# A graph layer and a mixture of experts on one core: seven stages to a row tile in place of ten, a new order of the three products and of the norms' shift, small loads of their own, and another way to the power of e

## The chip, the core and the metric

The kernel runs on one NeuronCore of a Trainium2 chip. The core has five engines with instruction queues of their own: PE (TensorE, matrix products), DVE (VectorE), ACT (ScalarE), POOL (GpSimd) and SP (SyncE, which here only issues DMAs). Each works through its queue in order and waits on semaphores for the others. A weight load of PE (PEld) can run beside a product. Sixteen DMA engines move data between HBM and the on-chip memory.

The metric is the device time of one execution in microseconds (us); lower is better. Times are medians of several runs. The profile is of one further execution, taken by the hardware profiler.

## What is computed

Two layers over 6,250 nodes with 512 features each, in f32. Cut to what matters:

```python
def gnn(x, src, dst):                       # x: layer-normed rows
    agg = segment_sum(x[src], dst)          # 106,250 edges, sorted by dst
    h = (agg / max(cnt, 1)) @ W_l.T + b_l + x @ W_r.T
    h = (h - mean(h, 0)) * rsqrt(var(h, 0) + EPS) * gamma + beta
    return relu(h) + x

def ffn(t):                                 # t: layer-normed rows
    logits = gelu(t @ Wg1 + bg1) @ Wg2 + bg2
    gates = softmax(logits)
    topv, topi = top_k(gates, 2)            # two of eight experts
    topv = topv / sum(topv)
    cw = sum(one_hot(topi) * topv)
    h = gelu(ln(t @ W1[e] + b1[e]) * g1[e] + be1[e])     # 512 -> 256, for each expert e
    h = gelu(ln(h @ W2[e] + b2[e]) * g2[e] + be2[e])     # 256 -> 256
    o = h @ W3[e] + b3[e]                                # 256 -> 512
    return sum_e(cw[:, e] * o[e])

x = x + gnn(layernorm(x), src, dst)
x = x + ffn(layernorm(x))
```

## The kernel before

**Graph layer.** Rows are normed and stored in HBM, gathered by edge with indirect DMAs (L636), summed per node by products with a selection matrix (L643), multiplied by W_l and W_r (L432) and stored as `d_d`. Column sums give the factors `bn_a` and `bn_b` of the norm over all nodes. Nothing of this is touched by the change.

**Expert layer.** The 49 token tiles of 128 nodes are cut into seven groups of seven. A token tile is loaded (`token_load`), scaled by `bn_a` and shifted by `bn_b` on DVE (`token_scale`, L822 and L823); its input row is normed on ACT (`token_shift`, L828); DVE adds the two and takes the statistics (`token_sum`, L834, L784, L785); ACT norms it (`token_norm`, L804); PE transposes it (`token_turn`, L846) and computes the gate's first product (`token_gate`, L855), ACT its gelu (L857), PE the logits (`token_logits`, L864). When a group has its logits, `route` chooses two experts for each token, computes their two weights with an exponential on ACT (L919, L920, L932 to L934), and assigns each token a row in a *row tile*: 128 rows of one expert in `xs_d`, 528 numbers each (512 features, the token's number, eight weights, padding). `send` scatters the rows there with indirect DMAs on POOL (L868). `route` is a generator in pieces, which are placed in chosen steps.

A full row tile is a *job*; up to 105 are provided for, 102 of them in the ordinary course and the last three behind a flag. Per job:

- `job_load` (L1071, SP): the row tile comes in, 128 x 528
- `job_turn` (L1077 to L1088): DVE copies the token numbers (`to`, as integers) and the weight of this expert (`cw`) out of the tile; PE transposes it in four parts; ACT copies the result to `xT`
- `layer(p, 0)` and `layer(p, 1)` (L1096, L1099, L784, L785): the product with W1 or W2 on PE, then on DVE the bias and the statistics of the norm
- `layer_norm` (L804, ACT), `layer_turn` (L1113 on PE, L1116 on ACT): the norm, its transposes, the gelu with gain and shift
- `job_product` (L1125, PE), `job_bias` (L1132, DVE), `job_weigh` (L1136, ACT): the product with W3, its bias, the weight
- `job_out` (L1140, POOL): an indirect DMA that adds the rows to `out`

**Order.** It is written out by hand in `run(s, ...)`: step s handles one stage each of several jobs and token tiles. `on(lag)` means job s - lag, `at(lag)` a token tile that entered `lag` steps ago. A job is transposed in step s; W1 follows in s + 1, the norm in s + 2, its transposes in s + 3, W2 in s + 4, norm in s + 5, transposes in s + 6, W3 in s + 7, bias and weighing in s + 8 and the scatter in s + 9. In a step's end PE runs W1, W2, W3 in this order. The order of the calls in `run` is the order in each engine's queue.

The statistics of a step's two layer outputs and its token tile lie together in one small tile `mv` of a `Step`. `scales()` adds the epsilon on DVE (L794) and raises to the power -1/2 on POOL (L795); `shifts()` computes minus mean times scale on DVE in the next step (L799). Both numbers feed ACT's norms (L804). In `run` the shifts stand behind `token_scale`, `token_shift` and `token_sum`.

Buffers: four tiles `xe`, fourteen of `to` and `cw`, three of `oe` (the output rows), three of `hn` for each layer; in PSUM three banks for transposes, two halves for W1 and W2 and one bank for W3. `no_tokens` fills a tile with zeros and the number 65536 (`OOB`), which the scatter leaves out; it is written to the empty slot `xs_d[SLOTS]` once (L1283).

Ahead of the steps `ahead` brings the first two groups of tokens through, without jobs beside them.

Of the kernel before, what the change touches and what calls it, by code (L numbers as in the profile page):

```python
# [28 lines left out]
def gnn_moe_kernel(ctx: ExitStack, tc: tile.TileContext, x, src, dst, wlT, b_l, wrT, gamma, beta,  # L29
# [736 lines left out]
    def no_tokens(a):  # L766

        nc.vector.memset(a, 0.0)
        nc.vector.memset(a[:, D:D + 1], OOB)
        return a  # L770

    JOBS = {}
# [47 lines left out]
    def token_scale(q, j):  # L820
        dt = tokens[q, j][1]
        nc.vector.tensor_mul(dt, dt, bn_a)  # L822
        nc.vector.tensor_add(dt, dt, bn_b)  # L823

# [57 lines left out]
    def route(q):  # L882
# [36 lines left out]
        nc.vector.tensor_tensor(s[:, 2:4], s[:, 0:2], s[:, None, 0].to_broadcast([P, 2, n]), op=OP.subtract)  # L919
        nc.scalar.activation(s[:, 2:4], s[:, 2:4], AF.Exp)  # L920
# [4 lines left out]
        nc.vector.tensor_copy(t2[:, :n, D], tok[:, g[0]:g[0] + n])  # L925
# [140 lines left out]
    def job_load(p):  # L1066
        sl, e = JOBS[p]
        at = nc.values_load(sl, engines=[SP_], min_val=0, max_val=SLOTS,
                            skip_runtime_bounds_check_because="a tile's number, or SLOTS")
        xe = sb.tile([P, RW], F32, name="xe", bufs=4)  # L1070
        ld = nc.sync.dma_start(xe, xs_d[ds(at, 1)].rearrange("o p c -> p (o c)"))  # L1071
        tc.add_to_no_dep_group("full", ld.ins)
        XE[p] = xe

    def job_turn(p):
        xe = XE.pop(p)
        e = nc.values_load(JOBS[p][1], engines=[PE_, DVE_, ACT_], min_val=0, max_val=E - 1,  # L1077
                           skip_runtime_bounds_check_because="an expert's number")
        to = sb.tile([P, 1], I32, name="to", bufs=14)
        cw = sb.tile([P, 1], F32, name="cw", bufs=14)  # L1080
        nc.vector.tensor_copy(to, xe[:, D:D + 1])
        nc.vector.tensor_copy(cw, xe[:, D + 1:D + 1 + E][:, ds(e, 1)])
        EV[p] = e, to, cw
        pt = ps.tile([P, KD, P], F32, name="pt", bufs=3)
        for k in range(KD):
            nc.tensor.transpose(pt[:, k, :], xe[:, k * P:(k + 1) * P], ident)  # L1086
        XT[p] = sb.tile([P, KD, P], F32, name="xT")
        nc.scalar.copy(XT[p], pt)  # L1088
# [49 lines left out]
    def job_out(p):  # L1138
# [4 lines left out]
        tc.add_to_no_dep_group("added", st.ins)  # L1143

# [51 lines left out]
    def run(s, prev, lo, hi, moves=False, do=(), late=()):  # L1196
# [73 lines left out]
    with tc.manual_schedule():  # L1270
# [95 lines left out]
        for s in range(MOST, MOST + 10):  # L1366
            prev = run(s, prev, 0, MOST)
    with tc.If(flag > 0), tc.manual_schedule():
        prev = Step()
        for s in range(MOST, SLOTS + 10):  # L1370
# [38 lines left out]
```

## Time and profile before

| | |
|---|---|
| time of the runs | 2033.29 us median of 3 (2033.22 to 2036.03) |
| the profiled execution | 2240.89 us, span 2239.1 us |
| granted clock of TensorE | 0.937 mean |
| graph layer | to about 1433 us |
| first two token groups | to 1514.0 us, when the first row tile is transposed |
| steps with jobs | 1514.0 to 2228.8 us (last scatter) |
| PE busy | 1925.0 us of the span; 647 of the 725 us from 1514.0 on |
| DVE, ACT, POOL busy | 1090.2, 666.7, 1208.0 us of the span |
| job scatter on POOL (L1140) | 102 of 1.63 us |
| power on POOL (L795) | 121 of 0.87 us |
| copies of numbers and weights on DVE (L1081, L1082) | 102 each of 0.154 us |
| table loads on ACT (L920, L1116, L857) | 7 + 5 + 3 of 1.28 us |

The profiled execution is 207.6 us longer than the median of the runs. How to read the profile: "busy" is the time in which an engine had an instruction of its own; a product of PE is counted to its modelled end. A row `PE pt L846 <- ACT t L804: 11.2, 5, 2.8` in the waits says that PE's transposes of line 846 waited for ACT's line 804 for 11.2 us in all, 5 times, 2.8 us at most. In the chain of waits a row is start, length and what. In a timeline it is start, length, engine, line and operation, and in brackets how long the engine was idle before it and what ended that. In the rows by stage ("windows") the busy times of PE, PEld, DVE, ACT and POOL come first, with the instructions in brackets, then the granted clock, the share of DMA and its GB/s.

### The profile page before, as it was taken

To read this page: it belongs to the slowest core of one execution; us is meant where nothing else is said; L and a number is where in the kernel's file an instruction comes from. 1 tells how busy PE (TensorE), PEld (TensorE's weight loads), DVE (VectorE), ACT (ScalarE), POOL (GpSimd) and SP (SyncE) were. 2 spreads that over 40 slices of the span, in tenths; PEclk is the share of its full clock that TensorE was granted. 3 is DMA by queue.
4 is the path that set the end of the run, shared out by engine and by line. 5 is a ranking of instruction groups with operands and counts; after the bars stand their busy time and mean duration, and the time that the engine had idled before them with its cause. 6 is when DMAs were issued, how large, how long until landed. Compare 5 with 4: busy or idle time off the path is not lost. (4 is left out here: it accounts for less than half of the span.)

```text
span 2239.1 us, 23976 instructions
## 1 busy us (share of the span) xinstructions
PE 1925.0 (86%) x6268; PEld 1048.7 (47%) x6268; DVE 1090.2 (49%) x2577; ACT 666.7 (30%) x1284; POOL 1208.0 (54%) x1229
## 2 busy tenths in 40 slices
PE   6867988889889988998988988657899999998993
PEld 2433433334334433444443443336676766766761
DVE  5642333333333333333333333477878787785652
ACT  3420000000000000000000000255676776765662
POOL 1346666556566666666666666143455454465342
PEclk9989999899999999999999999767999999999997
DMA  7876677666667777777877766465667676655542
GB/s 249 274 269 201 211 214 207 199 196 193 192 192 214 231 228 213 229 230 235 278 231 223 252 205 195 138 217 180 162 159 196 144 204 156 178 135 125 96 68 36
DMA packets 183185, 434.09 MB, mean 194 GB/s; under 512 B 32484, under 2 KB 38638, under 8 KB 182626
## 3 DMA queue, kind: packets, MB, share of 16 engines
q0 software_dynamic: 91040, 274.90, 45.4%
q1 hardware_dynamic: 91606, 156.69, 21.0%
q8 instruction: 56, 0.92, 0.2%
q10 hardware_dynamic: 396, 0.87, 0.1%
q14 instruction: 87, 0.71, 0.1%
HBM read 331.22 MB, written 104.20 MB: 194 GB/s over the span
## 5 line engine op out<-in xcount | busy, mean ns | idle before, releaser
L636 POOL DMA_INDIRECT xg<-xn_d,scol x832 | 790.1, 950 | 465.7 <-PE pa L643 198.4
L643 PE MATMUL pa<-xg,sel 128*128 128x512 f32 x1664 | 813.3, 612 | 21.6 <-issue 19.6
L643 PEld LDWEIGHTS pa<-xg,sel 128*128 128x128 f32 x1664 | 316.4, 197 | 378.0 <-issue 370.0
L1140 POOL DMA_INDIRECT out<-oe,to x102 | 166.7, 1634 | 189.4 <-DMA out<-oe,to 33.6
L507 DVE TENSOR_SCALAR rc<-pt 128x1 f32<-128x1 f32 x49 | 7.7, 158 | 474.4 <-PE pt L586 248.4
L432 PE MATMUL ph<-wl,xT 128*128 128x512 f32 x392 | 201.1, 596 | 14.4 <-issue 11.0
L1096 PE MATMUL pm<-w1s,xT 128*128 x816 | 207.6, 399 | 3.6 <-DVE hn L1099 3.6
L1125 PE MATMUL po<-w3s,hT 128*128 x408 | 198.0, 608 | 12.7 <-DVE oe L1132 12.5
L795 POOL TENSOR_TENSOR mv<-mv,mhalf 128x2 f32<-128x2 f32 (+2 forms) x121 | 105.6, 872 | 190.7 <-DVE mv L794 187.7
L562 DVE TENSOR_REDUCE ss<-sel 128x128 f32<-128x2304 f32 x49 | 199.4, 4069 | 0.5 <-issue 0.4
L528 ACT ACTIVATE sq<-dt 128x512 f32<-128x512 f32 x49 | 29.5, 602 | 569.2 <-issue 356.2
L432 PE MATMUL ph<-wr,xT 128*128 128x512 f32 x200 | 122.4, 698 | 68.7 <-ACT xT L427 45.8
L1096 PEld LDWEIGHTS pm<-w1s,xT 128*128 128x128 f32 x816 | 154.1, 199 | 23.8 <-DVE hn L1099 4.6
L1116 ACT ACTIVATE hT<-pt,gbe 128x128 f32<-128x128 f32 x408 | 153.9, 461 | 1.5 <-PE pt L1113 1.4
L567 ACT ACTIVATE ag<-pa,rc 128x512 f32<-128x512 f32 x49 | 33.7, 687 | 380.4 <-PE pa L643 263.6
L804 ACT ACTIVATE hn<-hn,mv 128x256 f32<-128x256 f32 x204 | 112.0, 601 | 101.7 <-DVE mv L799 101.1
L432 PEld LDWEIGHTS ph<-wl,xT 128*128 128x128 f32 x392 | 73.5, 190 | 113.5 <-issue 106.4
L556 DVE TENSOR_TENSOR sel<-jrow_p,dcol 128x2304 f32<-128x2304 f32 x49 | 124.4, 2539 | 0.0
L868 POOL DMA_INDIRECT xs_d<-t,pos x98 | 101.1, 1032 | 41.7 <-issue 25.0
L427 ACT COPY xT<-pt 128x512 f32<-128x512 f32 x74 | 43.3, 585 | 231.0 <-PE pt L425 64.7
L1125 PEld LDWEIGHTS po<-w3s,hT 128*128 128x128 f32 x408 | 76.1, 192 | 76.6 <-issue 54.4
L524 DVE TENSOR_TENSOR dt<-ph,xo 128x512 f32<-128x512 f32 x24 | 16.6, 691 | 189.1 <-issue 106.4
(307 smaller groups left out, 2236.3 us busy)
## 6 DMA issues: line engine op xcount, KB each, us to landing
xe<-xs_d SPq DMA_DIRECT2D x102, 264.0 KB
xg<-xn_d,scol POOLq DMA_INDIRECT x832
d_d<-dt SPq DMA_DIRECT2D x49, 256.0 KB
dt<-d_d SPq DMA_DIRECT2D x49, 256.0 KB
xt<-in_x SPq DMA_DIRECT2D x24, 512.0 KB
xn_d<-xt SPq DMA_DIRECT2D x24, 512.0 KB
xy<-y_d SPq DMA_DIRECT2D x48, 256.0 KB
xt<-in_x SPq DMA_DIRECT2D x48, 256.0 KB
```

The costliest lines, as they stand in the source:

```text
L432: nc.tensor.matmul(p, xT[:, k, :], w[:, k, :], start=start and k == 0, stop=stop and k == KD - 1)
L556: nc.vector.tensor_tensor(SEL[t], jrow_p[:, None, :].to_broadcast([P, KS, P]), dcol[:, t // TG, (t % TG) * KS:(t % TG + 1) * KS, None].to_ ...
L562: nc.vector.tensor_reduce(ss, SEL[t].rearrange("p k j -> p j k"), AX.X, OP.add)
L636: nc.gpsimd.indirect_dma_start(out=xg, out_offset=None, in_=xn_d[:, :], in_offset=bass.IndirectOffsetOnAxis(ap=scol[:, t // TG, c:c + 1], ...
L643: nc.tensor.matmul(PA[t], SEL[t][:, k, :], xg, start=(k == 0), stop=(k == last))
L795: nc.gpsimd.tensor_tensor(self.part[:, :, 1], self.part[:, :, 1], mhalf[:, :hi - lo], op=OP.pow)
L804: nc.scalar.activation(out_, in_, AF.Identity, bias=scale_shift[1], scale=scale_shift[0])
L868: st = nc.gpsimd.indirect_dma_start(out=xs_d.rearrange("n p c -> (n p) c"), out_offset=bass.IndirectOffsetOnAxis(ap=at, axis=0), in_=rows_ ...
L1096: nc.tensor.matmul(pm, lhs[:, k, :], w[:, k, ds(e, 1), :].rearrange("p o h -> p (o h)"), start=(k == 0), stop=(k == kk - 1))
L1116: nc.scalar.activation(hT[:, k, :], pt[:, k, :], AF.Gelu, bias=gb[:, 2 * i + 1:2 * i + 2], scale=gb[:, 2 * i:2 * i + 1])
L1125: nc.tensor.matmul(po, hT[:, k, :], w3s[:, k, ds(e, 1), :].rearrange("p o h -> p (o h)"), start=(k == 0), stop=(k == KH - 1))
L1140: st = nc.gpsimd.indirect_dma_start(out=out[:, :], out_offset=bass.IndirectOffsetOnAxis(ap=to[:, 0:1], axis=0), in_=OE.pop(p), in_offset=N ...
```

## The change

- A job passes in seven steps: W1 in the step of its transposes, W2 in the step of the first norm's transposes, W3 with bias and weighing one step behind the second norm's transposes, the scatter one step later. The last loops have 7 further steps in place of 10.
- In a step PE runs W3 (with its bias on DVE queued behind it), then W1, then W2; W3 comes ahead of the norms, W1 and W2 stay at the end.
- `token_scale` is split: `token_mul`, then both `shifts()`, then `token_add` and `token_sum`. On ACT `token_shift` comes behind the norms and the weighing.
- Numbers and weights of a job have a DMA of their own into a tile `ev` of 16 columns (14 buffers), and `xe` keeps the 512 features. The token's number is stored as an integer, so that the scatter reads it where it lies; ACT picks the expert's weight itself. The two DVE copies fall away.
- `route` needs one power for each token: e to the second logit minus the first, on POOL, with a tile full of e as the base; the first weight's numerator is 1.
- The empty tile is made in a buffer of the token rows (`t2s[1]`) in place of an `xe` tile.

```diff
     def no_tokens(a):
         nc.vector.memset(a, 0.0)
-        nc.vector.memset(a[:, D:D + 1], OOB)
+        nc.vector.memset(a[:, D:D + 1].bitcast(I32), int(OOB))
         return a
+    euler = wts.tile([P, GMAX], F32, name="euler")
+    nc.vector.memset(euler, 2.718281828459045)
...
-    def token_scale(q, j):
+    def token_mul(q, j):
         dt = tokens[q, j][1]
         nc.vector.tensor_mul(dt, dt, bn_a)
+
+    def token_add(q, j):
+        dt = tokens[q, j][1]
         nc.vector.tensor_add(dt, dt, bn_b)
...
-        nc.vector.tensor_tensor(s[:, 2:4], s[:, 0:2], s[:, None, 0].to_broadcast([P, 2, n]), op=OP.subtract)
-        nc.scalar.activation(s[:, 2:4], s[:, 2:4], AF.Exp)
+        nc.vector.tensor_sub(s[:, 3], s[:, 1], s[:, 0])
+        nc.gpsimd.tensor_tensor(s[:, 3], euler[:, :n], s[:, 3], op=OP.pow)
...
-        nc.vector.tensor_copy(t2[:, :n, D], tok[:, g[0]:g[0] + n])
+        nc.vector.tensor_copy(t2[:, :n, D].bitcast(I32), tok[:, g[0]:g[0] + n])
...
-        nc.vector.tensor_add(s[:, 0], s[:, 2], s[:, 3])
-        nc.vector.reciprocal(s[:, 1], s[:, 0])
-        nc.vector.tensor_tensor(s[:, 2:4], s[:, 2:4], s[:, None, 1].to_broadcast([P, 2, n]), op=OP.mult)
+        nc.vector.tensor_scalar(s[:, 0], s[:, 3], 1.0, None, op0=OP.add)
+        nc.vector.reciprocal(s[:, 2], s[:, 0])
+        nc.vector.tensor_mul(s[:, 3], s[:, 3], s[:, 2])
...
-        xe = sb.tile([P, RW], F32, name="xe", bufs=4)
-        ld = nc.sync.dma_start(xe, xs_d[ds(at, 1)].rearrange("o p c -> p (o c)"))
-        tc.add_to_no_dep_group("full", ld.ins)
-        XE[p] = xe
+        xe = sb.tile([P, D], F32, name="xe", bufs=4)
+        ev = sb.tile([P, RW - D], F32, name="ev", bufs=14)
+        for a, lo, hi in ((xe, 0, D), (ev, D, RW)):
+            ld = nc.sync.dma_start(a, xs_d[ds(at, 1), :, lo:hi].rearrange("o p c -> p (o c)"))
+            tc.add_to_no_dep_group("full", ld.ins)
+        XE[p] = xe, ev
...
-        to = sb.tile([P, 1], I32, name="to", bufs=14)
-        cw = sb.tile([P, 1], F32, name="cw", bufs=14)
-        nc.vector.tensor_copy(to, xe[:, D:D + 1])
-        nc.vector.tensor_copy(cw, xe[:, D + 1:D + 1 + E][:, ds(e, 1)])
-        EV[p] = e, to, cw
+        EV[p] = e, ev[:, 0:1].bitcast(I32), ev[:, 1:1 + E][:, ds(e, 1)]
...
-        for i, lag in ((0, 3), (1, 6)):
+        for i, lag in ((0, 2), (1, 4)):
             if on(lag):
                 layer_turn(s - lag, i)
-        if on(9):
-            job_out(s - 9)
-        if on(8):
-            job_bias(s - 8)
+        if on(6):
+            job_out(s - 6)
         if moves:
             if at(5):
                 token_logits(*at(5))
             if at(1):
-                token_scale(*at(1))
-                token_shift(*at(1))
+                token_mul(*at(1))
+        tprev.shifts()
+        prev.shifts()
+        if moves:
+            if at(1):
+                token_add(*at(1))
             if at(2):
                 token_sum(*at(2), step)
-        tprev.shifts()
-        prev.shifts()
-        for lag in (2, 5):
+        if on(5):
+            job_product(s - 5)
+            job_bias(s - 5)
+        for lag in (1, 3):
             if on(lag):
                 layer_norm(s - lag)
         if moves and at(3) and at(3) != normed_one:
             token_norm(*at(3))
-        if on(8):
-            job_weigh(s - 8)
+        if on(5):
+            job_weigh(s - 5)
+        if moves and at(1):
+            token_shift(*at(1))
         for f in do:
             f()
-        if on(1):
-            layer(s - 1, 0, step)
-        if on(4):
-            layer(s - 4, 1, step)
-        if on(7):
-            job_product(s - 7)
+        if on(0):
+            layer(s, 0, step)
+        if on(2):
+            layer(s - 2, 1, step)
...
-                no = sb.tile([P, RW], F32, name="xe", bufs=4)
-                nc.sync.dma_start(xs_d[SLOTS], no_tokens(no))
+                nc.sync.dma_start(xs_d[SLOTS], no_tokens(t2s[1][:, 0, :]))
...
-        for s in range(MOST, MOST + 10):
+        for s in range(MOST, MOST + 7):
             prev = run(s, prev, 0, MOST)
```

More of the change, by code (lines that the diff above doesn't have):

```diff
@@ L818, in token_load, with token_scale @@
         tokens[q, j] = xt, dt
-    def token_scale(q, j):
+    def token_mul(q, j):
         dt = tokens[q, j][1]
         nc.vector.tensor_mul(dt, dt, bn_a)
+    def token_add(q, j):
+        dt = tokens[q, j][1]
         nc.vector.tensor_add(dt, dt, bn_b)
+    def token_scale(q, j):
+        token_mul(q, j)
+        token_add(q, j)
     def token_shift(q, j):
@@ L1069, in job_load @@
                             skip_runtime_bounds_check_because="a tile's number, or SLOTS")
[L1070 to L1073 removed]
+        xe = sb.tile([P, D], F32, name="xe", bufs=4)
[4 more added lines that the diff above has]
+        XE[p] = xe, ev
     def job_turn(p):
[L1076 removed]
+        xe, ev = XE.pop(p)
         e = nc.values_load(JOBS[p][1], engines=[PE_, DVE_, ACT_], min_val=0, max_val=E - 1,
                            skip_runtime_bounds_check_because="an expert's number")
[L1079 to L1083 removed]
+        EV[p] = e, ev[:, 0:1].bitcast(I32), ev[:, 1:1 + E][:, ds(e, 1)]
         pt = ps.tile([P, KD, P], F32, name="pt", bufs=3)
@@ L1369, in gnn_moe_kernel @@
         prev = Step()
-        for s in range(MOST, SLOTS + 10):
+        for s in range(MOST, SLOTS + 7):
             prev = run(s, prev, MOST, SLOTS)
```

## The prediction

> **What bounds the kernel now.** I read the rows by stage first (the windows view), because the share of busy time over the whole span mixes two kernels: the graph layer up to about 1433 us, which the change does not touch, and the expert layer behind it. In the expert layer the steps that carry a job run from the first transposes of a row tile at 1514.0 to the last scatter at 2228.8.
>
> ```profile
> 1604.30:1990.00 385.70, 363.17 (x1743) 261.03 (x1742) 312.91 (x1052) 277.36 (x569) 197.34 (x170) 0.98 0.68 172
> 1990.00:2043.60 53.60, 45.24 (x197) 31.04 (x196) 32.12 (x113) 30.63 (x67) 38.76 (x36) 0.99 0.62 149
> 2043.60:2239.10 195.50, 160.95 (x670) 110.44 (x670) 95.49 (x307) 105.73 (x233) 75.34 (x63) 0.91 0.44 75
> ```
>
> The columns behind the length are PE, PEld, DVE, ACT, POOL busy, then the granted clock. In the middle PE is busy 363 of 386 us, so most steps are at PE's own pace. The chain of waits gives that pace: W1 begins at 1622.52, 1629.77 and 1637.03, so 7.25 us with a token tile; in the timeline the transposes of xe stand at 2062.00 and 2067.18, so 5.18 us without. Fourteen jobs and seven token tiles make 14 x 5.18 + 7 x 2.07 = 87.0 us of PE. But the chain shows one restart after a stall per group, at 1614.92, 1711.50, 1808.59 and 1904.53: 96.5 us apart. **9.5 us per group are not PE's work.** The waits of PE in 1604.3 to 1990 name them:
>
> ```profile
> PE pt L846 <- ACT t L804: 11.2, 5, 2.8
> PE pt L1113 <- ACT hn L804: 3.1, 3, 1.1
> PE pt L1086 <- issue: 3.1, 4, 1.2
> PE pm L1096 <- DVE hn L1099: 2.5, 2, 2.2
> PE po L1125 <- DVE oe L1132: 2.2, 5, 0.6
> ```
>
> 22.1 us in four groups, mostly for ACT's norms (L804). What makes ACT late stands in the chain itself:
>
> ```profile
> 1702.39 0.69 DVE oe L1132
> 1703.08 0.61 DVE dt L822
> ...
> 1703.72 0.69 DVE dt L823
> 1704.41 0.61 DVE xt L834
> ...
> 1705.04 0.71 DVE st L784
> 1705.75 0.02 issue
> 1705.77 0.07 DVE mv L785
> ...
> 1705.87 0.14 DVE mv L799
> ...
> 1706.04 1.09 ACT hn L804 x2
> 1707.13 0.71 ACT t L804
> ...
> 1707.89 1.01 PE pt L846 x4
> ```
>
> The 0.14 us shift (L799), which the norms need, stands on DVE behind 3.5 us of bias and token work, and PE's transposes wait at the end of that row. Last, POOL's timeline of the end:
>
> ```profile
> 2208.27 1.59 POOL L1140 DMA_INDIRECT out<-oe,to  x1 [3.26 <-ACT hT L1116]
> 2213.91 1.53 POOL L1140 DMA_INDIRECT out<-oe,to  x1 [4.05 <-DMA out<-oe,to]
> 2219.29 1.53 POOL L1140 DMA_INDIRECT out<-oe,to  x1 [3.85 <-DMA out<-oe,to]
> 2224.68 1.54 POOL L1140 DMA_INDIRECT out<-oe,to  x1 [3.85 <-DMA out<-oe,to]
> ```
>
> Each scatter into out is issued only when the one before has landed. From 2180.73 to 2224.68 that is 8 in 43.95 us, 5.49 us each, and from 2109.38 to 2155.24, with row tiles still being loaded, 5.73. This is slower than PE's 5.18: **from about 2109 on the end is set by how many scatters are left.**
>
> **The change part by part.**
>
> *Seven stages for ten.* A job's scatter goes out in the sixth step behind its transposes, where it was the ninth. No work is added or removed; 111 steps become 108. In the tail three more scatters are already out when the last job enters: 3 x 5.49 = **-16.5 us**. If the scatters did not bind, three drain steps would go all the same, at 4 to 5 us each by an estimate from PE's 5.18 with a job or more missing (13 us), so this part is safe within 4 us.
>
> *W3, W1, W2, and use in the same step.* W1 now needs xT of the same step, W2 needs hT of the same step. Cover: between the transposes of xe and W1 PE has those of hn (0.44) and W3 (1.72), 2.16 us, and ACT's copy takes 0.58, so 1.5 us are spare; the first two of the four gelus (1.51 for four) have W1's 1.74 us besides. W3 has its bias a whole step before the next W3, so the 2.2 us for "oe" go. In the first five steps W3 is not there yet and W1 waits about 0.6 us for the copy, 3 us at most; DVE paces these steps, so I cost it at nothing. W2 and W3 also come into the filling earlier, with their additions (1.05 us of DVE for one, 0.69 for the other) in 2 and 3 steps: +4.2 at most on DVE.
>
> *The shift ahead of the token work.* Multiply, then shifts, then add, sum and bias. Of the 3.5 us ahead of L799 only one 0.69 us operation is left, so ACT's norms come up to 2.8 us sooner; the longest stall was 2.8. On ACT the token's own shift (0.82) moves behind the norms and the weighing; its reader on DVE comes in the next step. On DVE the bias now waits for W3, and the routing pieces and both hn additions are queued behind it, which PE's next W1 and the norms need. In a token step DVE begins some 1.3 us after the end of W2 (addition and statistics of hn1) and has 3.2 us of token work, so it comes to the bias after 4.5; W3 ends after 0.44 + 0.98 + 0.59 + 0.44 + 0.31 + 1.72 = 4.5 us of PE. The wait is short. What is late next is DVE itself: 312.9 us busy of 385.7, with waits of only 13 us in a group of 97. I let the waits for t, hn and oe go, 11.2 + 3.1 + 2.2 = **-16.5 us**, and leave the other 5.6. Bounds: 0 to -22.
>
> *The clock behind the stalls.* In 1711.3 to 1716.0 the granted clock was 0.62, and twelve W1 and W2 matmuls took 4.32 us where full steps take 2.79. PE is busy 363.2 us in four groups whose work is 348, so 15 us are slow matmuls. The Trainium skill (TensorE: Matmul & The Clock Gate, "What's actually happening") lets the clock fall after an idle window of about 3.4 us; the waits of PE here are at most 2.8 us, and by that rule nothing slowed and nothing comes back: 0. The row shows that it slowed. I follow the row, but take half: **-8 us**.
>
> *Numbers and weights from a load of their own.* DVE loses two copies, 0.154 us each (102 + 102), which gives back 0.36 us per step in its order (1689.40 to 1689.76 in the timeline); this is what lets DVE follow PE and is not counted again. SP issues one more DMA a step (about 0.35 us; it idles), with rows of 64 bytes. "DMA: Bandwidth & Descriptors" ("Bandwidth") speaks against it: a transfer of 4 KB costs 0.68 us and small ones are all descriptors; an estimate of 0.7 us for each of some 20 loads beside binding scatters would be +14. The row: a whole 264 KB load delays a scatter by 5.73 - 5.49 = 0.24 us, so a 8 KB one by no more, at most +5. I take **+1.5**.
>
> *The power of e on POOL.* Seven exponentials on ACT and 15 table loads of 1.28 us (7 + 5 + 3) go: 19 us of an ACT that is busy 277 of 386. POOL gains seven powers of seven columns; by the rows (0.86 us at 2, 0.93 at 3, 1.04 at 4 columns) about 1.35 us each. The result is read a step later; POOL waits 83 us for DVE in the middle stage. Behind it on POOL stand the step's own power and then a scatter, which both wait for later work. Nothing, and -2 us ahead of the steps.
>
> *Filling and last group.* In 1514 to 1604 PE waits 8.8 us for ACT's t and hn and for oe; against the +4.2 above I take -3. In 1990 to 2043.6 PE waits 5.8 us for the first row tile of the last group, which stays, and 2.8 for hn and oe: -2.
>
> The empty tile written from another buffer and the integer in place of a float cost nothing: the same bytes, far from any wait.
>
> **Sum:** -16.5 - 16.5 - 8 + 1.5 - 2 - 3 - 2 = -46.5 us on an execution of 2240.9 (span 2239.1): about 2194. The runs shown have a median of 2033.3, 207.6 us less, and no view says where. If the gain shrinks with them (x 0.907) it is -42; if not, -46.5. I take -43: **1990 us**.
>
> **Rivals.**
> 1. *DVE stays the limit.* For it: DVE is busy 78 of 97 us in a group and waits 13, so with the gaps between instructions 84 us are its own. The stall then moves from the norms to the hn additions, and only the tail is won, with a few us of the rest: 2033 - 16.5 - 4 = **2013**. Against it: 0.36 x 14 = 5 us of DVE go per group.
> 2. *PE alone is left.* All four groups at 87: 4 x 9.5 = 38, tail 16.5, filling and last group 12: **1967**. Against it: routing makes single steps too long for DVE.
> 3. *Slower: W1 waits for ACT.* One mechanism: in token steps ACT ends with weighing, token shift, copy of tt and gelu, and only then copies xT. The timeline shows ACT idle 0.9 us ahead of xT in such steps, and the cover adds 1.5. If the token shift, now behind the weighing, which itself waits for the bias, makes ACT later by over 2.4 us, each of about 33 token steps pays the rest. At 3.9 us late that is 33 x 1.5 = 50, the groups' gain is lost, and the tail's remains: 2033 - 16.5 + 50 = **2067**. It makes the kernel slower than before from 2.9 us on. Against it: 5.92 us of ACT work in a step of 7.3.
>
> **The numbers.** Forecast 0.50, rival 1 0.18, rival 2 0.15, rival 3 0.17. About 4 us (0.2%) is what a measurement can tell from no change; I give 0.03 of rival 1 and 0.02 of rival 3 to that. Faster 0.80, same 0.05, slower 0.15. The range takes in the forecast, rival 2 with its bounds and most of rival 1: 1958 to 2032.
>
> **What would show it.** Groups of 14 jobs 89 to 92 us apart; no wait of the token transposes for ACT's t over 1 us; granted clock 1.00 in all steps from 1600 on; first scatter some 20 us earlier and the same 5.5 us between the last ones; no table load behind the first gelu. I am wrong if PE's W1 waits for ACT's xT, or DVE's hn waits vanish while PE's appear, or if the spacing of the last scatters grows with the small loads.

## The result, and the profile after

The changed kernel takes 2042.85 us (median of 15 runs, 2038.13 to 2051.72); the kernel before, on the same chip, 2033.29. The ratio is 1.0048, 95% interval 1.0034 to 1.0061. The prediction was 1990 us: the change costs about 9.6 us where it was to save 43. Here and below a ratio leaves out executions in a slower state of the chip, so it can differ by up to 0.4% from the quotient of two medians.

Two lengths show where the time went. From the first transposes of job 0 to those of job 77, the profile of before has 529.6 us (1514.0 to 2043.6), that of after 557.0 (1310.4 to 1867.4): 27.4 us more. From there to the end of the last scatter before has 186.7, after 168.8: 17.9 us less. The sum is +9.5. That it fits the times so well is luck: a second profile of the changed kernel gave 550.5 and 165.8, together 716.3 us, no longer than before, though that kernel's runs were slower again (1.0042). The expert part of single profiles varies by some 5 to 10 us, so the verdicts below rest on the times, and profiles tell where to look.

The view by stages, four groups of 14 jobs each. First before, the last row of the answer for jobs 14 to 70; then after, row by row. The columns behind the length are PE, PEld, DVE, ACT and POOL busy, then the granted clock.

```profile
sum 384.00, PE 365.02 PEld 262.12 DVE 312.35 ACT 276.69 POOL 197.40; mean PE 91.26 PEld 65.53 DVE 78.09 ACT 69.17 POOL 49.35
```

```profile
1411.50:1514.40 102.90, 94.18 (x441) 65.40 (x439) 73.93 (x234) 67.30 (x140) 53.52 (x45) 0.97 0.67 169
1514.40:1615.80 101.40, 92.80 (x440) 64.73 (x438) 74.64 (x234) 67.03 (x140) 49.87 (x44) 0.98 0.65 166
1615.80:1717.20 101.40, 91.68 (x440) 63.64 (x439) 74.72 (x234) 67.03 (x140) 51.16 (x44) 1.00 0.66 166
1717.20:1820.60 103.40, 93.04 (x437) 65.37 (x436) 75.02 (x250) 65.21 (x138) 51.45 (x46) 0.97 0.59 145
sum 409.10, PE 371.70 PEld 259.14 DVE 298.30 ACT 266.57 POOL 206.01; mean PE 92.92 PEld 64.79 DVE 74.58 ACT 66.64 POOL 51.50
```

A group takes 102 us, not the 89 to 92 of the prediction. DVE and ACT did lose work (312 to 298, 277 to 267 us), as the change says. But PE now stands still for 37.4 of 409.1 us, before for 19.0 of 384.0 (34.5 of 399.6 in the second profile). The engines that were thought late have less work, and PE waits more. (PE's busy time is 6.7 us longer too; the second profile does not show that, 365.1.) The waits of PE in these four groups of after:

```profile
PE pt L855 <- ACT t L806: 11.4, 12, 2.1
PE pt L1120 <- ACT tt L857: 9.8, 11, 1.7
PE pl L938 <- DVE t L935: 5.1, 4, 1.5
PE po L1132 <- DVE oe L1139: 3.8, 3, 1.3
PE pm L1103 <- DVE hn L1106: 3.5, 5, 2.3
PE pt L1120 <- ACT hn L806: 2.4, 8, 0.6
```

The wait for ACT's t, the first that was to go, is still there (11.4 us in 12 waits). A new one stands beside it: PE's transposes wait for ACT's copy tt, 9.8 us. Behind both are waits of DVE and of ACT, in the same stretch:

```profile
ACT hn L806 <- DVE mv L801: 65.5, 35, 4.9
...
DVE mv L801 <- POOL mv L797: 55.8, 46, 3.9
...
ACT oe L1143 <- DVE oe L1139: 33.9, 36, 2.8
...
DVE oe L1139 <- PE po L1132: 16.3, 8, 4.3
```

In before, over the same jobs, DVE's wait for the power and ACT's for the shift (lines 795 and 799 there) were shorter, and the two waits with oe did not show at all:

```profile
DVE mv L799 <- POOL mv L795: 4.9, 5, 1.4
...
ACT hn L804 <- DVE mv L799: 37.3, 24, 3.9
```

One step of after in the order of time:

```profile
1441.78 1.63 POOL L1147 DMA_INDIRECT out<-oe,ev  x1 [4.02 <-ACT oe L1143]
...
1442.88 0.17 DVE L796 TENSOR_SCALAR mv<-mv 128x3 f32<-128x3 f32 x1
...
1443.71 1.03 POOL L877 DMA_INDIRECT xs_d<-t,pos  x1 [0.30 <-issue]
...
1443.74 1.98 PE L1132 MATMUL po<-w3s,hT 128*128 x4
...
1445.04 0.99 POOL L877 DMA_INDIRECT xs_d<-t,pos  x1 [0.30 <-issue]
...
1446.03 0.93 POOL L797 TENSOR_TENSOR mv<-mv,mhalf 128x3 f32<-128x3 f32 x1
...
1446.99 0.17 DVE L801 SCALAR_TENSOR_TENSOR mv<-mv 128x3 f32<-128x3 f32 x1 [3.94 <-POOL mv L797]
...
1447.19 1.09 ACT L806 ACTIVATE hn<-hn,mv 128x256 f32<-128x256 f32 x2 [1.96 <-DVE mv L801]
...
1448.71 0.69 DVE L1139 TENSOR_TENSOR oe<-po,b3s 128x512 f32<-128x512 f32 x1
...
1449.04 0.66 PE L855 MATMUL pt<-identx,t 128*128 128x128 f32 x4 [0.73 <-ACT t L806]
...
1449.44 0.72 ACT L1143 ACTIVATE oe<-oe,ev 128x512 f32<-128x512 f32 x1 [0.45 <-DVE oe L1139]
```

DVE has the variance ready at 1443.05, but POOL has a scatter and two sends ahead of the power. The power comes at 1446.03, and the shift, now ahead of the token work, holds DVE for 3.94 us. ACT's norms wait 1.96 us for it, and PE's transposes of t 0.73 us in the end. This row is what first suggested the cause, and the experiments show that it was mostly not the cause. The same rows show the bias (L1139): W3 ends at 1445.72, DVE comes to its bias at 1448.71 without a wait for W3, and ACT's weighing (L1143) waits 0.45 us for that bias.

The tail did about what was predicted. The last scatters of after on POOL:

```profile
2014.63 1.59 POOL L1147 DMA_INDIRECT out<-oe,ev  x1 [3.33 <-ACT hT L1123]
...
2020.05 1.59 POOL L1147 DMA_INDIRECT out<-oe,ev  x1 [3.21 <-ACT hT L1123]
2025.31 1.54 POOL L1147 DMA_INDIRECT out<-oe,ev  x1 [3.67 <-issue]
2030.77 1.53 POOL L1147 DMA_INDIRECT out<-oe,ev  x1 [3.92 <-issue]
```

They still follow one another at 5.2 to 5.5 us. Three steps fewer saved 17.9 us here and 20.9 in the second profile, somewhat more than three such distances.

### The profile page after: what moved, and what is told of

It reads as the page before. It is cut to its first block, busy times and chain, and to the rows that moved or that the text cites. A ratio compares the mean times of both kernels' runs of the same rounds, so it can differ in the third digit from the quotient of the medians.

```text
span 2044.7 us, 24373 instructions
## 1 busy us (share of the span) xinstructions
PE 1864.5 (91%) x6268; PEld 1025.6 (50%) x6268; DVE 1060.8 (52%) x2370; ACT 649.1 (32%) x1263; POOL 1226.3 (60%) x1234
## 5 line engine op out<-in xcount | busy, mean ns | idle before, releaser
L643 PE MATMUL pa<-xg,sel 128*128 128x512 f32 x1664 | 789.9, 597 | 20.2 <-DMA y_d<-xg 18.5
L643 PEld LDWEIGHTS pa<-xg,sel 128*128 128x128 f32 x1664 | 306.5, 191 | 365.4 <-issue 349.1
L1147 POOL DMA_INDIRECT out<-oe,ev x102 | 167.8, 1645 | 155.0 <-ACT hT L1123 45.6
L1132 PE MATMUL po<-w3s,hT 128*128 x408 | 203.4, 622 | 6.0 <-DVE oe L1139 6.0
L1103 PE MATMUL pm<-w1s,xT 128*128 x816 | 198.9, 387 | 8.5 <-DVE hn L1106 6.7
L526 DVE TENSOR_TENSOR dt<-ph,shift 128x512 f32<-128x512 f32 x25 | 17.3, 692 | 192.3 <-PE ph L432 192.3
L1103 PE MATMUL pm<-w2s,hT 128*128 x408 | 105.9, 382 | 0.0
L432 PE MATMUL ph<-wr,xT 128*128 128x512 f32 x200 | 102.1, 592 | 0.0
```

The costliest lines, as they stand in the source:

```text
L432: nc.tensor.matmul(p, xT[:, k, :], w[:, k, :], start=start and k == 0, stop=stop and k == KD - 1)
L643: nc.tensor.matmul(PA[t], SEL[t][:, k, :], xg, start=(k == 0), stop=(k == last))
L1103: nc.tensor.matmul(pm, lhs[:, k, :], w[:, k, ds(e, 1), :].rearrange("p o h -> p (o h)"), start=(k == 0), stop=(k == kk - 1))
L1132: nc.tensor.matmul(po, hT[:, k, :], w3s[:, k, ds(e, 1), :].rearrange("p o h -> p (o h)"), start=(k == 0), stop=(k == KH - 1))
L1147: st = nc.gpsimd.indirect_dma_start(out=out[:, :], out_offset=bass.IndirectOffsetOnAxis(ap=to[:, 0:1], axis=0), in_=OE.pop(p), in_offset=N ...
```

## The experiments

In the first and third batch the chips gave 2229 and 2232 us for the kernel before, in the others 2032 to 2038; the extra 200 us lie in the graph layer. So a run is judged by its ratio to before on its own chip, and the intervals of the first and third batch are wider.

### First batch: one part undone at a time

The letters in the expectations name explanations of the loss; each is told where it first appears. The three parts other than the stages were put back one at a time, each as it was in before. The shift behind the token sum:

```diff
             if at(1):
                 token_mul(*at(1))
-        tprev.shifts()
-        prev.shifts()
-        if moves:
             if at(1):
                 token_add(*at(1))
             if at(2):
                 token_sum(*at(2), step)
+        tprev.shifts()
+        prev.shifts()
```

> The changed kernel with one part undone: the norms' shifts stand on DVE behind the token sum again (token multiply, add and sum first), all else stays. Changed kernel 2042.8, before 2033.3. Theory A (the shift, put ahead of the token work, makes DVE wait for POOL's power, which stands on POOL behind the scatters: 56 us in four groups that the token work hid before): groups of 14 jobs come back from 102 us to about 97, time 2015 to 2022. Theory B (the loss is in SP's and POOL's loop, by the second small load, or in W3's bias, and the place of the shift only moves the wait to another name): 2038 to 2050. If the shift ahead was a gain as predicted: 2055 or more.

One load of 528 columns per job, with DVE's two copies:

```diff
-        for a, lo, hi in ((xe, 0, D), (ev, D, RW)):
-            ld = nc.sync.dma_start(a, xs_d[ds(at, 1), :, lo:hi].rearrange("o p c -> p (o c)"))
+        ld = nc.sync.dma_start(xe, xs_d[ds(at, 1)].rearrange("o p c -> p (o c)"))
...
+        nc.vector.tensor_copy(to, xe[:, D:D + 1].bitcast(I32))
+        nc.vector.tensor_copy(cw, xe[:, D + 1:D + 1 + E][:, ds(e, 1)])
```

> The changed kernel with one part undone: one load of 528 columns per job and DVE's two small copies of it (token number, weights) as before, all else stays. Theory A (shift ahead of POOL): 2042 to 2052, since the two copies come back on DVE. Theory B (the second load on SP, 0.5 us of SP in a loop from the sends' landing over the row load and the token store to the next scatter): up to 0.5 us less in each of some 70 steps against 0.25 us more on DVE: 2015 to 2030.

The exponentials on ACT:

```diff
-        nc.gpsimd.tensor_tensor(s[:, 3], euler[:, :n], s[:, 3], op=OP.pow)
+        nc.scalar.activation(s[:, 2:4], s[:, 2:4], AF.Exp)
```

> The changed kernel with one part undone: the two exponentials of the gate on ACT again (with its table loads), the sum of both numerators on DVE; all else stays. Theory A (shift): 2040 to 2048, no change. Theory C (the power of e blocks POOL's queue until DVE's two maxima are there: 3.5 us in each of 5 groups, and PE waits 1.3 us for the routing product): 2025 to 2036.

And one edit that no part of the change made, on SP's queue. In both kernels the token store stands behind the loads of job rows:

```diff
-        loads(min(s + 4, hi))
+        loads(min(s + 1, hi))
         if on(0):
             job_turn(s)
...
                 token_sum(*at(2), step)
+        loads(min(s + 4, hi))
```

> The changed kernel with SP's order changed: a step's token store is issued ahead of the loads of job rows of that step, which wait on SP for the landing of the sends. The scatter of a job waits for the landing of the store of the step before (13.8 us of POOL waits in four groups, and what stands behind it). Theory A with this loop (late store, late scatter, late sends, late power, late shift, late store): the power comes 1 to 3 us earlier in most steps, 2015 to 2032. If the loop does not matter: 2040 to 2046.

Measured against before (2229.18 us there): shift back 2231.67, ratio 1.0021 (0.9997 to 1.0044); one load 2245.23, 1.0061 (1.0036 to 1.0085); exponentials on ACT 2237.79, 1.0030 (1.0009 to 1.0051); store first 2227.32, 0.9982 (0.9956 to 1.0008). Of the three undone parts, only the shift's interval leaves out the changed kernel's own 1.0048, and just so. That edit gave some 6 us where theory A (the early shift is the loss) expected 20 to 28, though its profile shows DVE's wait for the power down from 55.8 to 24.4 us:

```profile
DVE mv L801 <- POOL mv L797: 24.4, 27, 1.1
DVE oe L1139 <- PE po L1132: 13.8, 12, 1.7
...
DVE hn L1106 <- PE pm L1103: 12.9, 15, 1.1
```

Much of DVE's wait only changed its name. Theory B (the second load on SP) expected 13 to 28 us from the one load, and it is no faster; C (the power of e holds POOL) expected 7 to 18 us from ACT's exponentials, and gave some 4 with an interval that takes in none. The load order on SP was the one clear gain over the changed kernel (0.9982 against 1.0048); against before its interval does not exclude no change.

### Second batch: the stages alone

> The changed kernel itself, as a control beside the others: its expert part (first transposes of job 0 to the end of the last scatter) took 725.8 us in its one profile, 716.3 in the one of before. The graph layer ahead of it differs by tens of us between executions and between chips, so the expert part is what is compared. Expected: 723 to 729 us, ratio to before 1.003 to 1.006.

For the stages alone all three parts above were undone together.

> The changed kernel with three of its four parts undone: shifts behind the token sum, one load of 528 columns with DVE's two copies, exponentials on ACT. What is left is seven stages in place of ten, W3 ahead of W1 and W2. Theory A (the shift ahead is the loss, the others near nothing): expert part 705 to 717 us, thus not slower than before (716.3). Theory D (the seven stages themselves make the groups longer: the bias in the same step as its product, the gelu tiles needed at once): 718 to 730 us.

In the next one the two sends of a step go behind its power on POOL:

```diff
         step.scales()
+        for f in end:
+            f()
         return step
...
-                    put(do, a + j * (b + 1 - a) // g, send, q + 1, j)
+                    put(rows_late, a + j * (b + 1 - a) // g, send, q + 1, j)
```

> The changed kernel with the two sends of a step issued on POOL behind the step's power in place of ahead of it; the shift stays ahead of the token work, the scatter stays where it is. Theory A (DVE waits for a power that stands behind 2 x 1.0 to 1.3 us of sends): the 14 us per group of DVE's wait shrink in the steps with sends, expert part 706 to 718 us. If the power is late for another reason than what stands ahead of it on POOL: 722 to 728 us.

The last has the edit of SP's order above, made to the kernel before.

> The kernel before with only SP's order changed: token store ahead of the step's loads of job rows. In before the late store is hidden (POOL waits 5.3 us for it in four groups, DVE waits 4.9 us for the power). Theory A (the loop hurts only where the shift stands ahead of the token work): 712 to 717 us for the expert part, ratio 0.997 to 1.001. If the loop through the store cost before as much as it costs after: 690 to 700 us, ratio 0.990.

Measured (before 2032.16): the changed kernel again 2040.17, 1.0042 (1.0025 to 1.0058); **stages alone 2040.22, 1.0046 (1.0030 to 1.0062)**; sends behind 2045.98, 1.0068 (1.0051 to 1.0086); before with the store first 2026.76, 0.9970 (0.9960 to 0.9981).

The seven stages in their order, with a late shift, one load and ACT's exponentials, lose as much as the whole change: the other three parts together are worth nothing that this can tell. Theory A falls as the main cause, D (the seven stages in their order are the loss) stands. That rests on the times: the expert parts of the single profiles, 716.3 us for the changed kernel again and 715.1 for the stages alone, were expected at 723 to 729 and, by D, at 718 to 730; they missed both, and 715.1 lies in A's range. The waits in the groups of the stages alone, of DVE, PE and, in the last row, ACT:

```profile
DVE mv L801 <- POOL mv L797: 15.6, 31, 1.6
...
DVE oe L1141 <- PE po L1134: 14.2, 14, 1.7
DVE hn L1108 <- PE pm L1105: 13.4, 17, 1.5
...
PE pt L855 <- ACT t L806: 14.4, 10, 3.0
PE pt L1122 <- ACT hn L806: 8.7, 8, 2.6
PE pl L938 <- DVE t L935: 5.4, 4, 1.6
...
ACT oe L1145 <- DVE oe L1141: 2.8, 7, 0.4
```

Here DVE waits about a quarter as long for POOL, and PE still waits 14.4 us for t. ACT's wait for oe is down from 33.9 to 2.8 us, and the time is the same: that row of the changed kernel is not the loss by itself. With the sends out of the power's way DVE's wait for it fell only to 41.2 us, and a wait for the loads of d_d of 23.0 us came up: a miss for theory A too. The store ahead of the loads was expected to give 0 to 4 us on before by theory A, and about 20 if it cost as much there as in after; it gave 5.4. So the late store costs before as well, and there the row to see it in was DVE's 4.9 us for the power: with the store first it is gone.

### Third batch: W3 behind W2 again

If it is the order in the step, then it can be put back without giving up a stage, by taking W3's product one job earlier:

```diff
         if on(6):
             job_out(s - 6)
+        if on(5):
+            job_bias(s - 5)
...
-        if on(5):
-            job_product(s - 5)
-            job_bias(s - 5)
...
             layer(s - 2, 1, step)
+        if on(4):
+            job_product(s - 4)
```

The four runs are the stages alone and the whole change, each with this edit, without and with the store first.

> The seven stages alone (as in the run with the three other parts undone, ratio 1.0046), with one change: W3's product goes back behind W2's, one job earlier, and its bias opens the next step, so that it is still seven stages. Theory E (the order W3, W1, W2 puts W2's product last: it ends 6.1 us into a step of 7.1 in place of 4.2 of 6.9, and the chain from its end over DVE's statistics, POOL's power and the shift takes 4.1 us, so the next step waits for it): groups back to 95 to 97 us with the shorter tail kept, ratio 0.988 to 0.995 (2008 to 2022 us). Theory F (fewer stages as such: each product needs what ACT makes in the same step): groups stay at 98 to 102 us, ratio 1.002 to 1.008.

> The whole change, with W3's product behind W2's and the bias at the head of the next step (seven stages, shift ahead, small loads, power of e all kept). Theory E: DVE's wait for the power, 46 to 56 us in four groups, falls below 25, ratio 0.986 to 0.995. Theory A (the early shift behind POOL's scatters costs by itself, whatever stands behind W2): ratio 1.000 to 1.005, slower than the seven stages alone with W3 last. Theory F: 1.002 to 1.008.

> The whole change with W3 last, and the token store ahead of the step's loads on SP. Theory E, with the store's loop (6 us in before, 13 in the changed kernel): 5 to 13 us below the whole change with W3 last; ratio 0.982 to 0.990 (1997 to 2013 us). If the early store only helped where W2 is last: the same as the whole change with W3 last, within 3 us.

> The seven stages alone with W3 last, and the token store ahead of the step's loads on SP. Against the run before it shows what shift ahead, small loads and power of e together are worth with nothing in their way: predicted at some 20 us of gain, 0 to 5 by theory E (PE's busy time of 90 to 91 us per group limits both). Ratio 0.984 to 0.992.

Measured (before 2232.33): stages alone 0.9979 (0.9954 to 1.0004), whole change 0.9975 (0.9942 to 1.0007), whole change with the store first 0.9877 (0.9830 to 0.9924), stages alone with it 0.9901 (0.9863 to 0.9939). Seven stages as such are not the loss, so theory F (fewer stages, each needing ACT's result in the same step) falls: the same number of stages with W3 last is no longer slower. W1 does wait for ACT's xT now, as F and the prediction's third rival feared, but that is 7.8 to 11.2 us in four groups. Theory E (W2's product at the end of the step is the loss) had 0.995 or below for the first two, and they gain less; the two with the store first lie in its ranges. In the profile of the whole change with W3 last the stretch to job 77 is 529.4 us, that of before 529.6, and the tail 175.1: what this version gains, some 12 us by the profile, is the shorter tail alone, and that by less than in the changed kernel.

### Fourth batch: W3's place or its bias

That edit moved two things, W3 and the bias behind it. Each was to be moved alone: in the changed kernel the bias, weighing and scatter one step later; in the kernel before W3 alone ahead of W1.

```diff
+        if on(7):
+            job_out(s - 7)
         if on(6):
-            job_out(s - 6)
+            job_bias(s - 6)
...
         if on(5):
             job_product(s - 5)
-            job_bias(s - 5)
...
-        if on(5):
-            job_weigh(s - 5)
+        if on(6):
+            job_weigh(s - 6)
```

> The whole change with W3 left ahead of W1, and only the bias of its product (with the weighing and the scatter) a step later, so eight stages. Moving W3 last had moved the bias as well; this run moves the bias alone. Theory E (W2's product last in the step): no gain for the groups, one more step in the tail (5.5 us): ratio 1.004 to 1.009. Theory G (the bias waits for W3 in the same step and holds DVE, 16 us in four groups, and ACT behind it): groups 3 to 5 us shorter, ratio 0.995 to 1.001.

```diff
+        if on(7):
+            job_product(s - 7)
         for lag in (2, 5):
             if on(lag):
                 layer_norm(s - lag)
...
-        if on(7):
-            job_product(s - 7)
```

> The kernel before, ten stages, late shift, one load, exponentials on ACT, with one line moved: W3's product is issued ahead of W1's and W2's, as in the change. Theory E: W2 ends 2 us later in the step, groups of 14 jobs 3 to 5 us longer, ratio 1.007 to 1.012 (2047 to 2057 us). Theories F and G (fewer stages, bias in W3's step): 0.998 to 1.002, since the number of stages and the bias's place stay.

> The whole change with W3 last, again, to have it beside the two above on one chip: its ratio was 0.9975 with an interval of 0.994 to 1.001. Theory E: 0.990 to 0.998, 10 us or more below the run with the bias alone moved. Theory G: within 4 us of that run.

> The whole change with W3 last and the token store ahead of the row loads, again beside the others on one chip: ratio was 0.988 (0.983 to 0.992). Theory E with the store's loop: 0.984 to 0.992, the shortest of the four.

Measured (before 2032.28): bias alone 2159.39, 1.0618 (1.0601 to 1.0636); before with W3 ahead 2184.89, 1.0754 (1.0739 to 1.0769); W3 last 2026.19, **0.9968** (0.9956 to 0.9980); W3 last with the store first 2013.05, **0.9910** (0.9894 to 0.9927).

The first two are 127 and 153 us slower, which no theory had. One wait of PE says why, first in the run with the bias alone, then in that of before with W3 ahead:

```profile
PE po L1132 <- DVE oe L1139: 63.0, 41, 3.2
```

```profile
PE po L1125 <- DVE oe L1132: 63.8, 44, 2.6
```

W3 has one PSUM tile (po). With W3 early in a step and the bias at the head of the same step, for the job before, PE cannot begin W3 until DVE has got through the previous step's statistics to that bias. So, with one such tile, W3 ahead of W1 needs its bias in its own step, as the change has it. This does not tell theory E from G (the bias in the step of its product holds DVE, and ACT behind it).

### Fifth batch: W3 in the middle, and the shift once more

From the version with W3 last, W3 and W2 change places, and the bias stays at the head of the next step:

```diff
             layer(s, 0, step)
-        if on(2):
-            layer(s - 2, 1, step)
         if on(4):
             job_product(s - 4)
+        if on(2):
+            layer(s - 2, 1, step)
```

> The whole change with W3 last (ratio 0.9968), and of it only W3 and W2 changed over: W1, W3, W2 in a step, the bias at the head of the next step as there, a whole step part from its product less W2. So W2's product ends the step again, but no bias waits for a W3 just issued, and the PSUM tile of W3 is free in time. Theory E (W2's place at the end of the step is the loss): the gain is lost, ratio 1.001 to 1.008. Theory G (the bias in the step of its product is the loss): stays at 0.995 to 0.999.

The other run has W3 last and the store first, and the first batch's edit of the shift.

> The shortest version so far (whole change, W3 last, token store ahead of the row loads; ratio 0.991) with the norms' shift behind the token sum again. It shows what the shift ahead is worth where POOL's power is early (DVE waits 7 us for it in four groups). If it brings what was predicted (waits of PE for t, hn and oe gone, up to 16 us): 0.995 to 1.000. If it is worth nothing once the power is early: 0.990 to 0.993.

Measured (before 2037.55): W3 in the middle 2033.86, 0.9984 (0.9971 to 0.9997); shift back in the best version 2018.70, 0.9909 (0.9892 to 0.9925).

With W2 at the end of the step again, most of the gain is kept: 0.9984 against 1.0042 to 1.0048 of the changed kernel, 12 to 13 us, and 0.9968 with W3 last, 3 us more with intervals that overlap. So W2's place (theory E) is at most a small part: W2's product ends 6.2 us into the step here and 6.3 in the changed kernel, but 4.3 with W3 last (means of the four groups). What is gone is DVE's 16.3 us for po, and ACT's 33.9 us for oe. All waits of ACT in the groups with W3 in the middle, with no row for oe:

```profile
ACT xT L1095 <- PE pt L1093: 46.1, 45, 2.6
ACT hn L806 <- DVE mv L801: 38.6, 30, 2.7
ACT gts L866 <- PE pg L864: 17.8, 21, 2.7
ACT tt L857 <- PE pt L855: 10.9, 15, 1.5
ACT xT L1095 <- PE pt L1120: 4.5, 6, 1.1
ACT xT L1095 <- ACT gts L866: 0.3, 1, 0.3
```

The time lies in theory G's range, with two limits. First, the rows that G points to don't carry the loss by themselves: the stages alone lost as much with 2.8 us of ACT's wait, and DVE's idle time has other names here (18.6 us ahead of the bias with no releaser shown, 23.0 for W1 and W2 where the changed kernel had 4.6). Second, the edit also lets W1 begin 1.5 us into the step in place of 3.5, because W3 is no longer ahead of it; W1 begins at 3.3 to 3.5 in the changed kernel and in the stages alone, which lose, and at 1.3 to 1.5 in before and in all versions with W3 behind W1. W3 ahead of W1 together with its bias in the same step is shown to cost 12 to 13 us. How much of it is the bias and how much W1's lateness stays open: with one PSUM tile, W3 ahead without its bias cost 127 us and more.

The shift ahead is worth nothing that can be told: 0.9909 without, 0.9910 with it, in the version where the power is early (6.8 us of DVE's waits for it). The intervals leave room for some 5 us either way, not for 16.5.

### The version that beats both

W3 last with seven stages, and the token store ahead of the row loads: 2013.05 us against 2032.28, ratio 0.9910. Its groups, in the same view as above:

```profile
sum 372.00, PE 359.59 PEld 258.37 DVE 296.91 ACT 265.27 POOL 206.16; mean PE 89.90 PEld 64.59 DVE 74.23 ACT 66.32 POOL 51.54
```

93 us a group, PE idle 12.4 us in four, and the granted clock 1.00 in all four rows. All waits of PE that are left:

```profile
PE pm L1103 <- ACT xT L1095: 10.5, 32, 1.3
PE pt L1120 <- ACT tt L857: 0.6, 2, 0.5
PE pm L1103 <- DVE hn L1106: 0.5, 1, 0.5
PE po L1132 <- DVE mv L801: 0.2, 1, 0.2
```

The wait for t is gone. On W3 last alone, on the same chip, the store's place is worth 13.1 us, on the kernel before 5.4 us. The path, as far as the traces show it: SP issues in order, and in the four groups of after its row loads stood 147.8 us for the sends to land, in 25 waits; the store queued behind them is late, and the next scatter into out waits for it on POOL:

```profile
POOL out L1147 <- DMA out<-xt: 13.8, 7, 3.4
```

Behind that scatter stand the sends and the power, and the shift waits for the power. With the store first in the changed kernel, this row is gone and DVE's wait for the power is 38.8 us in place of 55.8; with it first in the version with W3 last, 6.8 in place of 25.7. In that version POOL's own row for the store did not fall (4.9 and 6.4 us), so by which wait the 13.1 us come there is not shown.

## Why the prediction was wrong, step by step

**The tail, -16.5: right.** 186.7 us became 168.8 and 165.8 in two profiles (-17.9 and -20.9), with 5.40 us between the last scatters where 5.49 was used. The first scatter came 50.5 us behind the first transposes of job 0, not 67.4: 17 us earlier, where 20 was said. With W3 last, where nothing else is lost, the tail is 174.3 to 175.1: about 12 us.

**"W3, W1, W2, and use in the same step", costed at nothing: this is the step that failed, and it made the change a loss.** It costs 12 to 13 us against W3 in the middle, and 15 to 16 against W3 last (0.9968 against 1.0042 to 1.0048). Had the order cost nothing, the change would have given about 6 us, not 43. Of the 52.6 us between forecast and result the order is thus some 15 to 16; nearly all the rest is gain that did not come, above all in the next two terms.

The step counted the cover of W1's wait for xT, and there it was right: no such wait in the four groups of after. The working in the next part then timed the bias against its W3 in a step with token work, found both at 4.5 us and concluded "The wait is short." For such steps this holds: in the 26 of them DVE never waits for W3, which ended 0.7 us or more before the bias began. What was left out is the rest. In steps without token work DVE does come too early: all 8 waits for po, 16.3 us, up to 4.3, lie there, two to a group. ACT's weighing waits for the bias in all 26 steps with token work, 27 of its 33.9 us. And W1 begins 3.5 us into the step in place of 1.3. The lengths of the steps, as means from one job's transposes to the next, say where to look (27 steps of the 56 with a token tile on PE, nearly the same as those with token work on DVE, and 29 without):

| | with token tile | without |
|---|---|---|
| before | 7.95 us | 5.84 us |
| after | 8.35 | 6.34 |
| after, second profile | 8.16 | 6.18 |
| stages alone | 7.98 | 6.22 |
| W3 in the middle | 7.84 | 6.05 |

With the stages alone nearly all the loss is in steps without a token tile, a kind of step for which the prediction did no such timing. These are single profiles; which of the three waits makes the loss is not shown.

**The shift ahead, -16.5: failed as well.** The chain row was read rightly, L799 behind 3.5 us of token work. The three waits of PE that were to go are 11.4 us for t, 2.4 for hn and 3.8 for oe, together 17.6 where before had 13.8 over the same jobs. The token work was also the cover of POOL's power: with part of it gone DVE stood 55.8 us for the power in place of 4.9. "What is late next is DVE itself" was wrong; late next was POOL, behind a scatter and two sends. POOL's queue ahead of the power was never timed against DVE's arrival at the shift. The runs give the early shift no worth: stages alone as slow as the whole change, and no difference in the best version. Nor did the waits of PE for t vanish with it. They went with the store above all: 3.0 us with the store first alone, 8.7 with W3 last alone, at most 0.6 with both.

**The clock, -8: failed with the waits it hung on.** Three of four groups of after show 0.97 or 0.98. In this choice between the row and the Trainium skill (TensorE: Matmul & The Clock Gate, "What's actually happening", an idle window of about 3.4 us) the row was right to be followed: PE's waits in these groups are at most 2.3 us and the clock still fell. Where the longest wait is 1.3 us it is 1.00 throughout, but so it is with the store first in the changed kernel, where it is 2.3: the longest wait alone does not decide. What was wrong was to expect the waits to go.

**Small loads, +1.5, and the power of e, -2: too small to be told.** One load again gave 1.0061, exponentials again 1.0030, both with the changed kernel's 1.0048 inside the interval. No run shows the +14 that was weighed for the small loads: putting the one load back gained nothing, though it brought DVE's two copies back with it. For the power, "nothing" behind it on POOL was not so: POOL stood 13.3 us in four groups for DVE's operand, in order ahead of its own power; no run shows a cost of it. The table loads did go, none behind the first gelu.

**Filling -3, last group -2.** Not seen. The first group takes 101.1 us (before 99.0); PE's waits for t, hn and oe are 7.0 us there where before had 8.8, but those for hn's addition, xT and others came on top, 14.2 in all. In the last part ahead of the tail, 46.8 us (before 46.6), PE waits 3.0 us for hn where hn and oe were 2.8.

**The profiled execution and the median.** Before's profile was 207.6 us above its median and no view of it said where. The profile of after shows it: job 0 begins at 1310.4 in place of 1514.0, 203.6 us earlier. Nearly all of it lies ahead of the expert layer, so the gain was not to be shrunk with it.

**The rivals.** The third had the sign, but not the mechanism: W1 never waited for xT in those groups. It came close in one place, ACT's weighing behind the bias, which it named as the way to be late; in the changed kernel tt's copy and PE's transposes were late behind it (9.8 us), not xT. The stages alone lose as much without that (0.8 us). The first rival's pace (groups at DVE's own 84 us) was not met either: DVE was busy 298 of 409 us.

## What to carry to other kernels

A shorter pipeline saves its gain in the tail, here 12 to 21 us for three steps; what it does to the middle has to be costed on its own. Before a wait is moved into the same step as its producer, time the arrival on both sides, in every kind of step and not only in the longest, and count all that is queued in order behind it, on the next engine too. When an operation is moved ahead of work that seemed to delay it, ask what the work was covering, and look at the in-order queue that makes its operand. And look for a store that sits behind a load with a wait: here the order of two issues on SP was worth 5 us in one kernel and 13 in another, more than all parts of the change that were aimed at DVE.

## What was not expected of the hardware

The same kernel took 2229 to 2232 us on the chips of two batches and 2032 to 2038 on those of the others, and the difference is in one layer alone: job 0 began at 1493 to 1523 us in the profiles of the first kind and at 1309 to 1313 in those of the second, while the expert part agreed within the scatter of its profiles (whole change with W3 last: 704.5 and 703.7 us). A share of a ratio's interval is thus from a layer that the change does not touch.
